# Four networks in a row on 4 x 56 x 56 x 128: spectra with an image in the input's tile, constant products in the later stages, bulk loads behind the first transform

## The chip, the cores and the metric

The kernel runs on one core of a Trainium2 chip, in one launch. A core has five engines that work side by side, each through its own list of instructions in order: TensorE (PE, matrix products; its weight loads are listed as PEld), VectorE (DVE), ScalarE (ACT), GpSimd (POOL) and SyncE (SP, which here only issues transfers). They meet through semaphores. TensorE's accumulators (PSUM) and the working memory (SBUF) hold 128 partitions each. The metric is the device time of an execution in microseconds (us).

## The reference

Four layers are applied to x (4, 56, 56, 128), each as `x = x + layer(groupnorm(x))`. Layer 0 is window attention, attention over all 3,136 tokens of a sample, and an MLP. Layer 1 is a graph layer over all pairs of 56 nodes. Layer 2 takes each of the 56 images of a sample (56 x 128) through a Fourier neural operator; layer 3 is a convolution over rows with sums along both axes. The change lies in layer 2, of which this matters:

```python
xa_n = _inorm(xa, norm_g[0], norm_b[0])                  # each image normalised
k = _fno_layer(xa_n, wK, wKs, bKs, (H // 2, W // 2))     # 32 heads each
q = _fno_layer(xa_n, wQ, wQs, bQs, (H // 2, W // 2))
v = _fno_layer(xa_n, wV, wVs, bVs, (H, W))
...
scores = jnp.einsum('bhtd,bhsd->bhts', qs, ks) / (np.sqrt(ks.shape[-1]).astype(np.float32) * TEMPERATURE)
attn_w = jax.nn.softmax(scores, axis=-1)                 # 56 x 56 per head and sample
out = jnp.einsum('bhts,bhsd->bhtd', attn_w, vs)
...
projd = _fno_layer(out, wP, wPs, bPs, (H, W))
attention = _inorm(projd + xa, norm_g[1], norm_b[1])
an = _inorm(attention, norm_g[2], norm_b[2])
m = _fno_layer(an, wM0, wM0s, bM0s, (H, W), (norm_g[3], norm_b[3]), act=True)
m = _fno_layer(m, wM1, wM1s, bM1s, (H, W), (norm_g[4], norm_b[4]), act=False)
output = _inorm(m, norm_g[5], norm_b[5]) + attention
```

where `_fno_layer` is a two-dimensional Fourier transform, a product with weights on the low frequencies, the transform back, and a skip path.

## The kernel before

**First layers.** Four samples run one after another (`first_layers`): a front (lines named f_, layer 0) and then the edge layer (e_, layer 1, `edge_layer`). The input of a sample lies in the tile xw (128 x 3136 numbers), the edge layer's result in x1. While a sample's front runs, group norm and image norm of the sample before it are done (`normed_images`), and its normalised images are stored to xad and, transposed, to xat in DRAM. For the last sample, number 3, that is left to the next stage, and its images stay in x1.

**Spectra** (`spectra`, L1699). Each sample's images pass a first transform in four quarters (`first_transform`: 28 pairs of thin products, s_pr, L1655; a multiplication by the image's own factor into s_z, L1657, on DVE; a copy on ACT, L1659). `sample_spectra` then makes from s_z the score spectra S and iS (s_ps, L1671, copies on ACT), the skip path's R (s_pr2, L1683) and the value spectra xh (s_px, L1693, copied in turn by ACT and DVE). It is a generator of 13 steps; between its steps the next sample's quarters are put (after steps 2, 5, 7 and 9), and steps of image 3's normalisation (`go_on`). That normalisation has 28 steps of two row statistics each, small products (s_pt, L1572 to L1615), two square roots, and four passes over the tile (`normed`, L1622, through `apply_norm`). The order on TensorE, ACT and DVE here is that of the code. `fill(n)` issues n products of the identity with ones (L1721), whose result nobody reads.

Images 0, 1 and 2 come from xad into tiles s_x2, of which there are two, and each transfer is issued on SP (`images`, L2933). SP takes its transfers in order: images 0 and 1, the store of x1 to x2d, small weights, the score weights (`all_score_weights`) and value weights (`value_weights`), image 2 when a tile is free, then dd, xat, the spectra's reordered copies (apart, q_T, q_Tp) and the first u_d. POOL computes with the weights meanwhile; the products of value weights go out as dd, which `attend` loads again as u_d.

**Score pass** (`attention_weights`, L1811). The samples are paired: bp = 0 is samples 0 and 1, bp = 1 samples 2 and 3. For each pair `seq` has 32 items (16 columns c, n = 0 and 1) and four odd items. `make` prepares an item's tile q_u: on DVE for n = 0 (L1864), on POOL for n = 1 (L1862). `product` (L1877) multiplies it, 16 records on TensorE, into q_acc. `make` runs four items ahead. `collect` adds q_acc to the scores y (L1896). The skip products and the softmax of the first pair are generators in `between`, one step after each item. A softmax step is a reduction, a subtraction, a reduction, a reciprocal and a multiplication on DVE (L1902 to L1911), an exponential on ACT, and transposes on TensorE (q_pt, L1919) that ACT copies to AT.

**Attend** (L1955) multiplies dd into the spectra (u_ud on DVE, L2018; u_up on POOL, L2020) and TensorE sums over AT (u_po, L2023), in 24 turns. Other work is put between, among it the second pair's softmax.

**Outputs** (L2777 on) hold the mixed FNO layers and layer 3. Their instructions are made as operations of a `Plan` and issued in an order written out by hand (OUTPUT_ORDER). The plan only asserts that dependences and the counted buffers are kept; tiles come from `bank()` and `banks()`.

Of the kernel before, what the change touches and what calls it, by code (L numbers as in the profile page):

```python
# [19 lines left out]
P = 128  # L20
# [1531 lines left out]
def normed_images(k, w, st, b, wk, bank, xp, xad, xat):  # L1552
# [48 lines left out]
    nc.vector.tensor_scalar(mean, mean, 0.5, mr[:, 0:1], ALU.mult, ALU.subtract)  # L1601
    nc.vector.tensor_scalar_mul(mean, mean, mr[:, 1:2])
    yield
    nc.vector.tensor_scalar(sq, sq, mr[:, 1:2], mr[:, 1:2], ALU.mult, ALU.mult)
# [37 lines left out]
def first_transform(k, st, b, pools, x, to):  # L1642

    nc = k.nc
    wk, psum = pools

    z = to[b] = wk.tile([P, 33, 2 * HH], F32, name="s_z")
    xf = x.rearrange("p t h -> p (t h)")  # L1650
    for t0 in range(0, HH, 14):
        ps = psum.tile([P, 512], F32, tag="row", name="s_pr")
        for t in range(14):
            for ri in range(2):
                nc.tensor.matmul(ps[64 * ri:64 * ri + 64, t * 33:(t + 1) * 33],  # L1655
                                 xf[:, (t0 + t) * HH:(t0 + t) * HH + 64], k.fw[:, ri, :], start=True, stop=True)
# [41 lines left out]

def spectra(k, w, st, xat, images):  # L1699

# [6 lines left out]
    with ExitStack() as es:  # L1707
# [6 lines left out]
        zs = {}  # L1714
        first = [first_transform(k, st, b, (wk, psum), st.x1 if b == B - 1 else images(b), zs) for b in range(B)]
        idle = tiny.tile([P, 512], F32, name="s_pt")
# [94 lines left out]
def attention_weights(k, I, w, st):  # L1811
# [9 lines left out]
    with ExitStack() as es:  # L1821
# [127 lines left out]
def attend(k, I, w, st, dd, xat, xm, softmax, beside, psum):  # L1949
# [4 lines left out]
    with ExitStack() as es:  # L1954
# [14 lines left out]
        def prepare(turn):  # L1969
# [18 lines left out]
            else:  # L1988
# [15 lines left out]
                 (1, 6): (mixing,), (2, 14): (mixing,), (2, 6): (mixing,), (2, 2): (mixing,), (3, 14): (mixing,)}  # L2004
        late = []
        prepare(0)
        for turn, (g, n, bp) in enumerate(turns):
# [5 lines left out]
            for i in range(2):  # L2013
                for h0, m, e in (shares if turn else first)[left < 16]:
# [6 lines left out]
                    for q in range(m):  # L2021
                        for b2 in range(2):
                            nc.tensor.matmul(po[64 * b2:64 * b2 + 64, :NB],  # L2023
                                             st.AT[:, 8 * i + h0 + q, 2 * bp + b2, :], u[:, b2, q, :],
                                             start=(left == 16), stop=(left == 1))
# [150 lines left out]


class Plan:

# [3 lines left out]
    def __init__(self, **buffers):  # L2183
        self.ops, self.buffers = [], buffers

# [7 lines left out]
    def issue(self, order):  # L2193
# [7 lines left out]
        for n in order:  # L2201
            op = self.ops[n]
            assert all(a.end for a in op.after)
            for b, key in op.takes:
                taken[b].append(key)
                old = len(taken[b]) - 1 - self.buffers[b]
                assert old < 0 or not users[b, taken[b][old]]
            op.run()
            op.end = True
            for g in op.gives:  # L2210
                users[g] -= 1


# [555 lines left out]
def outputs(k, w, st, ys, x2d, xm, out, psum):  # L2769

    tc = k.tc
    with ExitStack() as es:
        pools = Env()
        pools.wk = es.enter_context(tc.tile_pool(name="o_wk", bufs=2))
        opened, taken = [], [0]

        def bank():  # L2777
            return psum.tile([P, 512], F32, tag="b", name="o_b")

        def banks():  # L2780
            taken[0] += 1
            tag, bufs = ("x", 1) if taken[0] % 3 == 0 else ("px", 2)
            return psum.tile([P, 2, 512], F32, tag=tag, name="o_d", bufs=bufs)
        pools.bank, pools.banks = bank, banks
# [19 lines left out]
        for b, op in ((1, wholes[3].spread[0]), (2, wholes[3].factors)):  # L2804
            for p in wholes[b].convolve:
                p.after.append(op)
        plan.issue([int(n) for n in OUTPUT_ORDER.split()])

# [28 lines left out]
def build(k, packs, I, out):  # L2837
# [3 lines left out]
    with ExitStack() as es:  # L2841
# [8 lines left out]
        x1w = x1p.tile([P, HH + 1, HH], F32, name="x1")  # L2850
        x1 = x1w[:, :HH, :]
        dd = dp.tile([3, 4, 2, 16, NB], F32, name="dd")

# [4 lines left out]
        with tc.tile_pool(name="w01", bufs=1) as wp, tc.tile_pool(name="io", bufs=1) as io:  # L2858
            xw = io.tile([P, TOK], F32, name="xw")
            with ExitStack() as pre:  # L2860
# [52 lines left out]
            with small.Else():  # L2913
# [4 lines left out]
                with tc.tile_pool(name="n_x", bufs=2) as xs, tc.tile_pool(name="n_ps", bufs=2, space=PSUM) as psum:  # L2918
                    for b in range(B - 1):
                        xp = xs.tile([P, HH, HH], F32, name="n_x")  # L2920
                        nc.sync.dma_start(xp, x2d[b])
                        for _ in normed_images(k, w2, st, b, io, lambda: psum.tile([P, 512], F32, name="n_ps"), xp,
                                               xad, xat):
                            pass

        x2s = ExitStack()
        x2p = x2s.enter_context(tc.tile_pool(name="x2", bufs=2, side="right"))

        def images(b):
            if b not in loaded:  # L2930
                xp = loaded[b] = x2p.tile([P, HH + 1, HH], F32, name="s_x2")
                for o in (slice(0, 29), slice(29, HH)):
                    nc.sync.dma_start(xp[:, o, :], xad[b, :, o, :])  # L2933
                nc.gpsimd.memset(xp[:, HH, :], 0.0)
            return loaded[b]

        loaded = {}
        for b in range(2):
            images(b)
        nc.sync.dma_start(x2d[B - 1], x1)  # L2940
        l3p = es.enter_context(tc.tile_pool(name="l3", bufs=1))
        load_weights(k, l3p, I, "w3_", w2)
        load_weights(k, l3p, I, "w2_", w2, only=CONV_WEIGHTS)
        st.AbT = l3p.tile([P, 2, HH], F32, name="AbT")
        st.dc = l3p.tile([1, B, HH], F32, name="dc")
        with tc.tile_pool(name="xh", bufs=1) as xp:
            st.xh = xp.tile([112, B, 2, 32, HH], F32, name="xh")
            with tc.tile_pool(name="sp", bufs=1) as sp:
# [4 lines left out]
                with tc.tile_pool(name="g_wk", bufs=1, side="right") as wk:  # L2953
                    all_score_weights(k, I, w2, sp, wk, st)
                    value_weights(k, I, w2, wk, dd)
                    spectra(k, w2, st, xat, images)
                x2s.close()
# [35 lines left out]
```

## Time and profile before

| | us |
|---|---|
| median of 3 runs (least and greatest) | 3463.82 (3462.63 to 3465.51) |
| the profiled execution | 3464.84 |
| its span in the trace | 3463.1 |
| last edge stage ends, images 0 and 1 are issued | 2586.65 |
| first product of the spectra (constant) | 2588.75 |
| first product of the score pass | 2671.28 |
| first product of its second pair | 2733.92 |
| first u_po of attend | 2806.60 |

The span runs from the first instruction to the last; an execution is 1.7 us longer than it. The table's lower rows are starts on TensorE (for the images, on SP's queue), in us from the start of the span. In rows of the profile, `out<-in` are tile names, `x` counts records, and the mean or total follows in us. A product of 32-bit numbers can be more than one record on TensorE: a constant product over 384 columns has two. "Granted clock" (PEclk) is the share of TensorE's full clock that the chip allowed in a stretch, 1.00 being full speed.

### The profile page before, as it was taken

The page shows a single profiled execution, that of the slowest core. Times are in us where ns is not written, and L with a number is a line of the kernel's source. Part 1 is how long each engine was busy: PE and PEld are TensorE (multiplying, and loading weights), DVE is VectorE, ACT ScalarE, POOL GpSimd, SP SyncE. Part 2 cuts the span into 40 slices and gives each one's busy share as a digit, 9 for nine tenths or more (in the row PEclk, how much of TensorE's full clock was granted, in tenths as well). Part 3 has the DMA queues.
Part 4 walks back from the last instruction along what each step waited for, and adds up shares of the span by engine and source line. Part 5 has one row for each costly group of instructions (what it writes and reads, how often), then busy time and mean ns, then how long its engine had stood idle before and what let it go on. Part 6 is the DMA issues. An engine that isn't in the chain of part 4 may idle for free. (4 is left out here: it accounts for less than half of the span.)

```text
span 3463.1 us, 64456 instructions
## 1 busy us (share of the span) xinstructions
PE 3319.0 (96%) x27800; PEld 1425.6 (41%) x27800; DVE 2657.9 (77%) x2555; ACT 2131.1 (62%) x2253; POOL 1285.9 (37%) x796
## 2 busy tenths in 40 slices
PE   7999999999999999999999999999999999999998
PEld 4433333353333435333343443333337433336664
DVE  6588867867888696788859858887794778895776
ACT  4688876668888575788857668887653012215442
POOL 1000007800000491000019400000775778884786
PEclk9999999999999999999999999999999999999999
DMA  2143420024434000444310033442014037743101
GB/s 106 43 94 89 97 54 19 20 53 93 92 91 86 19 1 20 106 103 91 91 42 1 20 81 90 93 97 54 1 40 118 1 87 187 190 115 94 57 20 56
DMA packets 98012, 243.41 MB, mean 70 GB/s; under 512 B 64457, under 2 KB 69833, under 8 KB 92713
## 3 DMA queue, kind: packets, MB, share of 16 engines
q0 software_dynamic: 16128, 102.77, 14.8%
q1 hardware_dynamic: 74872, 123.61, 12.2%
q10 hardware_dynamic: 6720, 12.85, 1.3%
q8 instruction: 220, 3.60, 0.4%
q14 instruction: 72, 0.58, 0.1%
HBM read 79.43 MB, written 31.33 MB: 32 GB/s over the span
## 5 line engine op out<-in xcount | busy, mean ns | idle before, releaser
L830 ACT ACTIVATE f_ring<-f_pm 128x1792 f32<-128x1792 f32 (+1 forms) x764 | 1093.8, 1482 | 226.4 <-PE f_pm L827 179.6
L682 DVE TENSOR_TENSOR f_acc<-f_acc,f_ring 128x1792 f32<-128x1792 f32 x468 | 947.5, 2025 | 190.2 <-ACT f_ring L830 160.0
L827 PE MATMUL f_pm<-f_qT,f_kT 32*128 32x448 f32 x5376 | 722.6, 571 | 9.9 <-ACT f_p L716 4.1
L672 POOL DMA_DIRECT2D f_far<-f_ring x112 | 96.5, 862 | 1328.2 <-ACT f_ring L830 1033.4
L693 PE MATMUL f_pm<-f_ring,f_va 128*32 128x448 f32 (+1 forms) x6304 | 589.4, 490 | 0.0
L1269 POOL TENSOR_TENSOR e_tp<-e_a,e_c 128x1792 f32<-128x1792 f32 (+2 forms) x172 | 480.4, 2831 | 36.7 <-issue 36.7
L1267 DVE TENSOR_TENSOR e_td<-e_a,e_pc 128x1792 f32<-128x1792 f32 (+2 forms) x292 | 478.3, 1703 | 8.8 <-ACT e_c L1255 8.8
L827 PEld LDWEIGHTS f_pm<-f_qT,f_kT 32*128 32x128 f32 x5376 | 260.2, 183 | 411.5 <-ACT f_ring L830 300.3
L693 PEld LDWEIGHTS f_pm<-f_ring,f_va 128*32 128x32 f32 x6304 | 163.8, 109 | 410.1 <-issue 397.8
L1271 ACT ACTIVATE e_tp<-e_tp 128x1792 f32<-128x1792 f32 (+2 forms) x172 | 253.3, 1495 | 98.0 <-POOL e_tp L1269 98.0
L2018 DVE TENSOR_TENSOR u_ud<-u_px,u_d 112x1792 f32<-112x1792 f32 x144 | 263.4, 1863 | 39.7 <-PE u_po L2023 35.1
L2020 POOL TENSOR_TENSOR u_up<-xh,u_d 112x1792 f32<-112x1792 f32 (+1 forms) x72 | 240.9, 3373 | 55.0 <-PE u_po L2023 40.7
L1338 PE MATMUL e_acc<-e_td,t_edge 128*32 128x448 f32 x1952 | 231.6, 542 | 6.6 <-DVE e_td L1267 6.4
L2023 PE MATMUL u_po<-u_ud,AT 112*64 112x448 f32 x1056 | 213.9, 544 | 1.9 <-DVE u_ud L2018 1.9
L1338 PE MATMUL e_acc<-e_tp,t_edge 128*32 128x448 f32 x1184 | 147.9, 543 | 23.7 <-ACT e_tp L1271 23.7
L2023 PEld LDWEIGHTS u_po<-u_ud,AT 112*64 112x64 f32 x1056 | 74.3, 138 | 128.9 <-issue 112.8
L1338 PEld LDWEIGHTS e_acc<-e_td,t_edge 128*32 128x32 f32 x1952 | 61.6, 110 | 142.6 <-issue 93.7
L737 DVE RECIPROCAL f_den<-f_den 128x448 f32<-128x448 f32 x28 | 82.6, 2951 | 44.9 <-ACT f_den L734 44.9
L1862 POOL TENSOR_TENSOR q_u<-iS,q_g 128x1792 f32<-128x1792 f32 x32 | 102.8, 3235 | 22.8 <-PE q_acc L1877 22.8
L813 POOL TENSOR_TENSOR x<-xf,xw 128x343 f32<-128x343 f32 x28 | 25.5, 911 | 224.7 <-DVE xf L802 224.7
L1877 PE MATMUL q_acc<-q_u,S 64*64 64x448 f32 x1024 | 104.4, 552 | 4.4 <-DVE q_u L1864 3.3
L2121 ACT COPY x_ev<-x_po 56x896 f32<-56x896 f32 x32 | 28.8, 900 | 126.9 <-DMA x_xs<-xat 51.1
(525 smaller groups left out, 4579.1 us busy)
## 6 DMA issues: line engine op xcount, KB each, us to landing
f_far<-f_ring POOLq DMA_DIRECT2D x112, 896.0 KB, 6.4
u_d<-dd SPq DMA_DIRECT2D x46, 784.0 KB
f_far<-f_ring SPq DMA_DIRECT2D x28, 896.0 KB
xw<-in_x SPq DMA_DIRECT2D x4, 1568.0 KB
x2d<-x SPq DMA_DIRECT2D x4, 1568.0 KB
xat<-x SPq DMA_DIRECT2D x4, 1568.0 KB
x_xs<-xat ACTq DMA_DIRECT2D x32, 196.0 KB
xm<-x_ev ACTq DMA_DIRECT2D x64, 98.0 KB
```

The costliest lines, as they stand in the source:

```text
L682: nc.vector.tensor_add(e.acc, e.acc, slots(j, c))
L693: nc.tensor.matmul(e.po[heads[h], part], va[o, c, heads[h]], p, start=(c == 0), stop=(c == 23 and part.stop == NB))
L827: nc.tensor.matmul(ss[:, i, :NB], kT[heads[h], c * P:(c + 1) * P], qT[heads[h], blk(j)], start=True, stop=True)
L830: nc.scalar.activation(ring[:, slot:slot + m, :], ss[:, :m, :NB], AF.Exp, scale=scale)
L1267: nc.vector.tensor_tensor(t, am, cm, ALU.max)
L1269: nc.gpsimd.tensor_sub(t, am, cm)
L1271: nc.scalar.activation(tf, tf, AF.Relu)
L1338: nc.tensor.matmul(acc[quarters[r0 + r], :NB], w.S[:, 0, :], t[:, r].rearrange("p l n -> p (l n)"), start=(g == 0), stop=(g == len(turns) ...
L1877: nc.tensor.matmul(acc[bp][i][halves[hb % 2], hb // 2, :NB], x[o], u[o, 8 * hb:8 * hb + 8, :].rearrange("p h t -> p (h t)"), start=first, ...
L2018: nc.vector.tensor_mul(u, bc(px[:, :, :NB], 2, m), dm)
L2020: nc.gpsimd.tensor_mul(u, bc(x, 2, m), dm)
L2023: nc.tensor.matmul(po[64 * b2:64 * b2 + 64, :NB], st.AT[:, 8 * i + h0 + q, 2 * bp + b2, :], u[:, b2, q, :], start=(left == 16), stop=(left ...
```

## The change

1. The tile xw becomes 57 rows high and outlives the first layers. Image 0 is loaded into it from xad when the last sample's front has read it (`first_image`), and image 2 after image 0's first transform. Image 1 has the only s_x2 tile. `first_transform` asks for its tile when it starts.
2. In the spectra, image 0's four quarters stand first, with one fill(4) after the third; the steps of image 3's normalisation are put between the steps of the samples. Its four passes over the tile are done by ACT for sample 3 (`b == B - 1`).
3. `bulk`, called after the first transform, holds the score and value weights, the store x2d and the small weights, in that order on SP; image 2 is ahead of them.
4. The score pass begins with four constant products. In the first pair, POOL's items come one pair later. The first pair's softmax takes its steps at items n with n % 4 == 2 and n > 38 only.
5. Attend begins with four constant products, and has two more in turn 0.
6. In the outputs eleven constant products are issued: with the tile of operation n (FILL_OWN), or with a tile of their own ahead of it (FILL_SPARE).

```diff
     def normed():
         for t in range(0, HH, 14):
-            apply_norm(k, x[:, t:t + 14, :], x[:, t:t + 14, :], mr)
+            if b == B - 1:
+                nc.scalar.activation(x[:, t:t + 14, :], x[:, t:t + 14, :], AF.Identity, bias=t1, scale=mr[:, 1:2])
+            else:
+                apply_norm(k, x[:, t:t + 14, :], x[:, t:t + 14, :], mr)
...
-        fill(3)
-        go_on(28)
-        next(first[0])
-        next(first[0])
-        go_on(1)
-        fill(4)
-        next(first[0])
-        go_on(1)
-        next(first[0])
-        go_on(2)
+        for n in range(4):
+            next(first[0])
+            if n == 2:
+                fill(4)
+        images(2)
+        bulk()
         for b in range(B):
             for n, _ in enumerate(sample_spectra(k, st, b, (wk, psum), zs.pop(b))):
-                go_on(2)
+                go_on(4 if b == 0 and n < 7 else 2 if b and n > 8 else 1)
...
             for c in range(16):
-                seq += [(bp, c, 0, None), (bp, c, 1, None)]
+                seq.append((bp, c, 0, None))
+                if bp or c:
+                    seq.append((bp, c - (not bp), 1, None))
                 if c in (8, 10, 12, 14):
                     seq.insert(len(seq) - 1, (bp, None, c // 2 % 2, c // 12))
+            if not bp:
+                seq.append((bp, c, 1, None))
...
         ahead = 4
+        idle = psum.tile([P, 512], F32, tag="t", name="q_idle", bufs=1)
+        for _ in range(4):
+            nc.tensor.matmul(idle[:, :3 * P], k.ident, bc(k.ones, 1, 3), start=True, stop=True)
...
-            if n >= 3 and between and next(between[0], 0) == 0:
+            if n >= 3 and between and (item[0] == 0 or n % 4 == 2 and n > 38) and next(between[0], 0) == 0:
                 between.pop(0)
...
+        idle = bank()[:, 0, :3 * P]
+        def fill(n):
+            for _ in range(n):
+                nc.tensor.matmul(idle, k.ident, bc(k.ones, 1, 3), start=True, stop=True)
+        fill(4)
         prepare(0)
...
+                    if not turn and left == 15:
+                        fill(2)
...
+FILL_OWN = {42: 1, 82: 1, 330: 1, 743: 2, 748: 2}
+FILL_SPARE = {30: 1, 160: 1, 273: 2}
...
+            if n in FILL_SPARE:
+                self.idle = FILL_SPARE[n]
+                taken["b"].append(("idle", n))
...
+                self.spare()
+            self.idle = FILL_OWN.get(n, 0)
             op.run()
...
+        def filled(t, out):
+            for _ in range(plan.idle):
+                k.nc.tensor.matmul(out, k.ident, bc(k.ones, 1, 3), start=True, stop=True)
+            plan.idle = 0
+            return t
...
         with tc.tile_pool(name="w01", bufs=1) as wp, tc.tile_pool(name="io", bufs=1) as io:
-            xw = io.tile([P, TOK], F32, name="xw")
...
+            def first_image():
+                nc.sync.dma_start(xi[:, :HH, :], xad[0])
+                nc.gpsimd.memset(xi[:, HH, :], 0.0)
...
                 front(k, w0, xw, xf, x1, st)
+                if to is None:
+                    first_image()
                 edge_layer(k, w1, x1, st)
...
-        x2p = x2s.enter_context(tc.tile_pool(name="x2", bufs=2, side="right"))
+        x2p = x2s.enter_context(tc.tile_pool(name="x2", bufs=1, side="right"))
...
-                xp = loaded[b] = x2p.tile([P, HH + 1, HH], F32, name="s_x2")
+                xp = loaded[b] = xi if b == 2 else x2p.tile([P, HH + 1, HH], F32, name="s_x2")
...
-        loaded = {}
-        for b in range(2):
-            images(b)
-        nc.sync.dma_start(x2d[B - 1], x1)
+        loaded = {0: xi}
+        images(1)
         l3p = es.enter_context(tc.tile_pool(name="l3", bufs=1))
-        load_weights(k, l3p, I, "w3_", w2)
-        load_weights(k, l3p, I, "w2_", w2, only=CONV_WEIGHTS)
...
+                    def bulk():
+                        all_score_weights(k, I, w2, sp, wk, st)
+                        value_weights(k, I, w2, wk, dd)
+                        nc.sync.dma_start(x2d[B - 1], x1)
+                        load_weights(k, l3p, I, "w3_", w2)
+                        load_weights(k, l3p, I, "w2_", w2, only=CONV_WEIGHTS)
```

More of the change, by code (lines that the diff above doesn't have):

```diff
@@ L1602, in normed_images @@
     nc.vector.tensor_scalar_mul(mean, mean, mr[:, 1:2])
+    if b == B - 1:
+        nc.vector.scalar_tensor_tensor(t1, mr[:, 0:1], -1.0, mr[:, 1:2], ALU.mult, ALU.mult)
     yield
@@ L1621, in normed @@
         for t in range(0, HH, 14):
-            apply_norm(k, x[:, t:t + 14, :], x[:, t:t + 14, :], mr)
+            if b == B - 1:
+                nc.scalar.activation(x[:, t:t + 14, :], x[:, t:t + 14, :], AF.Identity, bias=t1, scale=mr[:, 1:2])
+            else:
+                apply_norm(k, x[:, t:t + 14, :], x[:, t:t + 14, :], mr)
             if t < 42:
@@ L1649, in first_transform @@
     z = to[b] = wk.tile([P, 33, 2 * HH], F32, name="s_z")
-    xf = x.rearrange("p t h -> p (t h)")
+    xf = x().rearrange("p t h -> p (t h)")
     for t0 in range(0, HH, 14):
@@ L1696, in sample_spectra, with spectra @@
         yield
-def spectra(k, w, st, xat, images):
+def spectra(k, w, st, xat, images, bulk):
     nc, tc = k.nc, k.tc
@@ L1714, in spectra @@
         zs = {}
-        first = [first_transform(k, st, b, (wk, psum), st.x1 if b == B - 1 else images(b), zs) for b in range(B)]
+        first = [first_transform(k, st, b, (wk, psum), lambda b=b: st.x1 if b == B - 1 else images(b), zs)
+                 for b in range(B)]
         idle = tiny.tile([P, 512], F32, name="s_pt")
@@ L2175, in conv_weights @@
     yield
+FILL_OWN = {42: 1, 82: 1, 330: 1, 743: 2, 748: 2}
+FILL_SPARE = {30: 1, 160: 1, 273: 2}
 class Plan:
     def __init__(self, **buffers):
-        self.ops, self.buffers = [], buffers
+        self.ops, self.buffers, self.idle, self.spare = [], buffers, 0, None
     def add(self, engine, cost, run, after=(), takes=(), gives=(), lag=0.0, table=None):
@@ L2207, in issue @@
                 assert old < 0 or not users[b, taken[b][old]]
+            if n in FILL_SPARE:
+                self.idle = FILL_SPARE[n]
+                taken["b"].append(("idle", n))
+                users["b", ("idle", n)] = 0
+                old = len(taken["b"]) - 1 - self.buffers["b"]
+                assert not users["b", taken["b"][old]]
+                self.spare()
+            self.idle = FILL_OWN.get(n, 0)
             op.run()
@@ L2211, in issue @@
                 users[g] -= 1
+            assert not self.idle
 def half_sample(k, w, st, plan, b, half, whole, pools, rows, x2d, xm):
@@ L2775, in outputs @@
         opened, taken = [], [0]
+        def filled(t, out):
[3 more added lines that the diff above has]
+            return t
         def bank():
-            return psum.tile([P, 512], F32, tag="b", name="o_b")
+            t = psum.tile([P, 512], F32, tag="b", name="o_b")
+            return filled(t, t[:, :3 * P])
         def banks():
@@ L2782, in banks @@
             tag, bufs = ("x", 1) if taken[0] % 3 == 0 else ("px", 2)
-            return psum.tile([P, 2, 512], F32, tag=tag, name="o_d", bufs=bufs)
+            t = psum.tile([P, 2, 512], F32, tag=tag, name="o_d", bufs=bufs)
+            return filled(t, t[:, 0, :3 * P])
         pools.bank, pools.banks = bank, banks
@@ L2806, in outputs @@
                 p.after.append(op)
+        plan.spare = bank
         plan.issue([int(n) for n in OUTPUT_ORDER.split()])
@@ L2851, in build @@
         x1 = x1w[:, :HH, :]
+        xwp = x1s.enter_context(tc.tile_pool(name="xw", bufs=1, side="right"))
+        xi = xwp.tile([P, HH + 1, HH], F32, name="xw")
+        xw = xi[:, :HH, :].rearrange("p t h -> p (t h)")
         dd = dp.tile([3, 4, 2, 16, NB], F32, name="dd")
@@ L2924, in build @@
                             pass
+                first_image()
         x2s = ExitStack()
[L2927 removed]
+        x2p = x2s.enter_context(tc.tile_pool(name="x2", bufs=1, side="right"))
         def images(b):
             if b not in loaded:
[L2931 removed]
+                xp = loaded[b] = xi if b == 2 else x2p.tile([P, HH + 1, HH], F32, name="s_x2")
                 for o in (slice(0, 29), slice(29, HH)):
                     nc.sync.dma_start(xp[:, o, :], xad[b, :, o, :])
[L2934 removed]
+                if b < 2:
+                    nc.gpsimd.memset(xp[:, HH, :], 0.0)
             return loaded[b]
[L2937 to L2940 removed]
+        loaded = {0: xi}
+        images(1)
         l3p = es.enter_context(tc.tile_pool(name="l3", bufs=1))
[L2942 to L2943 removed]
         st.AbT = l3p.tile([P, 2, HH], F32, name="AbT")
@@ L2953, in build @@
                 with tc.tile_pool(name="g_wk", bufs=1, side="right") as wk:
-                    all_score_weights(k, I, w2, sp, wk, st)
-                    value_weights(k, I, w2, wk, dd)
-                    spectra(k, w2, st, xat, images)
+                    def bulk():
[4 more added lines that the diff above has]
+                        load_weights(k, l3p, I, "w2_", w2, only=CONV_WEIGHTS)
+                    spectra(k, w2, st, xat, images, bulk)
                 x2s.close()
```

## The prediction

> **What bounds the kernel now.** I read the page's busy shares first, then the chain, then a table of the stretches that the change touches, then TensorE's waits there, and the granted clock last.
>
> ```profile
> span 3463.1 us, 64456 instructions
> PE 3319.0 (96%) x27800; PEld 1425.6 (41%) x27800; DVE 2657.9 (77%) x2555; ACT 2131.1 (62%) x2253; POOL 1285.9 (37%) x796
> ```
>
> TensorE is busy 96% of the span, so a gain must come from work taken off it, from its few idle stretches, or from its clock. Windows over the five stretches that the diff touches (start:end and length in us; busy time of PE, PEld, DVE, ACT, POOL; granted clock; DMA share; GB/s): spectra, first half of the score pass, second half, attend, outputs.
>
> ```profile
> 2588.00:2668.00 80.00, 75.89 (x1222) 65.25 (x1222) 37.20 (x113) 31.19 (x69) 35.27 (x53) 0.96 0.47 143
> 2668.00:2733.00 65.00, 61.51 (x816) 29.59 (x816) 46.16 (x26) 2.60 (x5) 57.04 (x19) 0.97 0.14 33
> 2733.00:2801.50 68.50, 61.58 (x560) 27.60 (x560) 50.17 (x32) 5.96 (x8) 45.90 (x15) 0.95 0.00 1
> 2801.50:3122.50 321.00, 316.19 (x1768) 117.84 (x1768) 277.94 (x172) 68.49 (x103) 267.01 (x91) 0.99 0.64 156
> 3122.50:3463.00 340.50, 314.71 (x2234) 205.02 (x2232) 226.41 (x398) 144.36 (x207) 222.59 (x136) 0.98 0.20 58
> ```
>
> The reader is to see a busy TensorE at a clock below 1.00: part of that busy time is slow time. What it waits for, by total, times and longest:
>
> ```profile
> PE q_pt L1919 <- DVE y L1911: 5.9, 1, 5.9
> PE q_acc L1877 <- DVE q_u L1864: 3.3, 1, 3.3
> PE u_po L2023 <- POOL u_up L2020: 2.4, 1, 2.4
> PE u_po L2023 <- DVE u_ud L2018: 1.9, 1, 1.9
> ```
>
> And the clock in short windows, same columns:
>
> ```profile
> 2608.00:2612.00 4.00, 2.91 (x50) 2.67 (x50) 1.37 (x5) 0.82 (x3) 2.99 (x8) 0.83 1.02 411
> 2612.00:2616.00 4.00, 4.00 (x38) 3.94 (x35) 1.36 (x3) 1.11 (x2) 3.80 (x6) 0.50 0.66 257
> 2672.00:2676.00 4.00, 4.00 (x28) 1.61 (x22) 4.00 (x3) 0.00 (x0) 4.00 (x2) 0.57 0.77 171
> 2744.00:2748.00 4.00, 0.98 (x4) 0.69 (x4) 3.97 (x3) 0.00 (x0) 2.02 (x1) 0.50 0.00 0
> 3400.00:3402.00 2.00, 2.00 (x16) 0.76 (x12) 0.26 (x2) 0.30 (x1) 2.00 (x2) 0.50 0.00 0
> 3416.00:3418.00 2.00, 2.00 (x4) 0.96 (x3) 1.41 (x4) 0.00 (x0) 2.00 (x2) 0.54 0.00 0
> ```
>
> Narrowing such windows, every change of clock lies a whole number of 3.413 us from every other. Half speed holds in 2610.67–2617.4, 2672.09–2675.5, 2743.75–2750.55, 2805.2–2812.0, 3399.1–3402.5 and 3416.2–3419.6. A half-speed window in which TensorE is the bound costs 1.7 us, half of 3.41.
>
> **Rule against row.** The Trainium skill, "TensorE: Matmul & The Clock Gate", section "Why this matters for your kernels", says that one idle window throttles the clock and warns of idle gaps above some 3 us. By it only the gap before 2747 would go cold, and constant products in short gaps would be useless work. The trace differs: in the windows ahead of the drops TensorE was busy 2.08 (2607.26), 0.83 (2668.69), 0.78 (2740.37), 0.97 (2801.81), 2.33 (3395.71) and 2.15 us (3412.78); others with 1.71 to 2.47 stayed fast. I take the row: a window about half filled is at risk. By the rule, the clock terms below (3.4 + 1.2 + 1.7 = 6.3) drop out, and the sum is −14.2 instead of −20.5.
>
> **1. Spectra, −8.** These lines (start, length, engine, line, operation) are the beginning now:
>
> ```profile
> 2588.75 2.17 PE L1721 MATMUL s_pt<-c_ones,t_shared 128*128 128x384 f32 x6 [0.94 <-PE e_idle L1298]
> 2591.72 3.46 PE L1655 MATMUL s_pr<-t_images,s_x 128*64 128x33 f32 x112 [0.80 <-DMA s_x<-xad]
> ```
>
> Six constant records wait out image 0's transfer, issued at 2586.65 when the edge stage ends. The change sends images 0 and 1 (1,568 KB each) under the last edge stage. Earlier batches load as much there, so I cost that at 0; uncovered it is some 5 us (2586.65 to 2591.72).
>
> Removed: fill(3), 2.17, the 0.80 wait, and the normalisation of image 3 ahead of the second quarter. New work of TensorE from 2588.7: 16 quarters at 1.755 (28.1), one fill(4) at 2.8, 256 columns' s_px at 0.103 (26.3), s_ps 4 x 1.75 (7.0), s_pr2 4 x 1.0 (4.0), norm products 1.0: 69.2. The hand-over from the last s_z to s_ps was 0.73 and stays; about 1 us of small waits I keep. It ends at 2659.6, against 2667.97: −8.3. I take −8, since four normalisations move to ACT (its 128x896 copy took 0.95, 128x448 0.53, so some 0.83 each) among the xh copies that TensorE waits for. In the list 3.4 comes from the two slow windows and 1.1 from `s_pt L1615 <- DVE s_sq`.
>
> What moves: image 2 now waits for the third and fourth quarter (about 2596.5, 2598.5), and is needed around 2617; it took about 5 us when issued alone, so it is hidden. SP's bulk loads stand behind it. POOL's weight work (2605.6 to 2642.9) must be complete for the score pass and dd before u_d's loads (2672): at a start of 2600 to 2606 there are 20 us to spare. The store xat waits for ACT (about 2635); behind it on SP stand apart, q_Tp and later u_d, the first needed 25 us later. The new normalisation spreads POOL- and DVE-side waits over samples 0 and 1. Bounds: −4 (image 2 or ACT late) to −10 (all small waits gone).
>
> **2. Beginning of the score pass, −1.2.** Four q_idle products fill the 3.3 us in which q_u is made: 2.8 us, ending about 0.1 after q_u is ready. The slow window (2672.09, 1.7) goes; TensorE then catches up with DVE's second product (0.4 lost). Bounds −1.7 to +1.
>
> **3. Second half, −9.3.** DVE's softmax for the first half of the heads is issued at every item in a row, so the transposes (q_pt) wait 5.9 at 2741 to 2747 and the next 3.4 run slow. The change gives it eight turns, at items 42 to 70, and no POOL-side product is delayed by them. Work for TensorE: 512 product records at 0.094 (48.1), odd items 4 x 1.66 (6.6), transposes 2.3, small waits 1: 58.2 against the 67.45 from 2733.9 to 2801.35. DVE does 30 us of products in this time (15 of 2.02) plus the softmax, about 4.6 per pair of b2 (reduce 1.08, subtract 1.09, reduce 1.08, reciprocal 0.25, multiply 1.09): stepped by hand, it stays 1.8 us ahead. The one multiply beside POOL took 2.68 instead of 1.09; two such use that lead up. Bounds −4.5 to −10.
>
> **4. Attend, 0.** fill(4) waits for the second collect (DVE, 2803.43) and would end at 2806.3, where u_po starts now (2806.60); fill(2) ends at 2808.1. DVE gives the next u_ud then, and at 2814.7 TensorE waits for DVE in both orders, so a faster clock is not kept. Bounds −0.5 to +1.
>
> **5. Outputs, −2.** The eleven extra products go into gaps of 0.66 to 1.34 us, each 0.70, two pairs slightly over (0.3). 3416's slow window goes (1.7), and I count half of 3399's at 0.6. Bounds −3 to +3.
>
> The third item of the score pass's order (POOL's second product one pair later) changes who waits by less than 0.3; its cover is `ahead = 4`.
>
> **Sum**: −8 −1.2 −9.3 +0 −2 = −20.5 on the profiled execution, 3464.84 (span 3463.1 and 1.7 around it): 3444.3. The median of the runs shown is 1.0 lower: 3443.3, put at **3443.5**.
>
> **Rivals.** (B) DVE becomes the bound in the second half: its share there is 50.17 of 68.50, and in 58 us it would be 86%. For it: 2.68 where 1.09 was enough. Against it: the 1.8 us lead. Gain 4.5 instead of 9.3: 3448.5. (C) The spectra gain half, because image 2, ACT's copies or the first load (DMA share 1.02 at 2608) are late: 3447.5. (D) The output products push the chain: each on the path costs 0.7, and the phase of the 3.413 us grid shifts by the gains upstream, so other gaps may fall into one window. Outputs +3 instead of −2: 3448.5. (E) The slower end: the spectra run at half speed throughout, because thin products (33 and 112 columns) count too little. Place: 2588 to 2660, 21 windows at 1.7. It decides from 12 windows (20.5 / 1.7); 16 make it slower by 0.2%, 21 give 3443.5 + 36 = 3479. For it: the window with 2.08 busy at 2607 fell, and fill(3) is gone ahead of the transforms. Against it: 2617 to 2668, the same mix, 15 windows at full clock. That images still arrive late, so that the first part does not do what it says, would cost 5 and is within (C).
>
> **Numbers.** Forecast 0.62, B 0.13, C 0.12, D 0.06, E 0.03, smaller unnamed losses that leave less than 0.2% 0.04. About 6.9 us (0.2%) is what a measurement can tell from no change. B, C and D alone stay faster; two together leave 10 to 12 of gain. So faster 0.93, same 0.04, slower 0.03. The forecast's bounds (spectra −10, outputs −3, second half −10) reach 3438; B to D end at 3448.5, and half of another miss at 3452: range 3438 to 3452.
>
> **What would show it.** Right: s_pr first at 2588.7 with no constant product ahead, first s_ps near 2599; clock 1.00 in 2588–2660 and at the score pass's beginning; no q_pt wait above 1 us; second half about 58; the stage's end near 2783; outputs about 338. Wrong: a wait of s_pr for image 2, of s_ps for ACT's normalisation, of q_acc for q_u at items 42 to 70, or a half-speed window behind a gap in the outputs that was fast before.

## The result and the profile after

| | before | changed |
|---|---|---|
| median of 14 runs (least and greatest), us | 3464.64 (3461.41 to 3465.73) | 3456.99 (3451.65 to 3464.92) |
| span of the profiled execution, us | 3463.1 | 3453.9 |
| mean granted clock there | 0.993 | 0.996 |

The ratio of the runs is 0.9981, with a 95% interval of 0.9973 to 0.9988. The change gains 7.7 us where 20.5 were forecast. The first lines of the page of the changed kernel:

```profile
span 3453.9 us, 64526 instructions
PE 3325.2 (96%) x27836; PEld 1429.8 (41%) x27836; DVE 2659.6 (77%) x2552; ACT 2134.5 (62%) x2257; POOL 1285.0 (37%) x795
```

The same five stretches as a table of windows of the changed kernel, with the columns of the table before:

```profile
2588.00:2665.00 77.00, 71.68 (x1220) 61.62 (x1218) 36.85 (x111) 34.98 (x74) 34.78 (x57) 1.00 0.50 129
2665.00:2729.50 64.50, 62.85 (x826) 30.30 (x826) 46.82 (x27) 2.38 (x5) 56.28 (x19) 1.00 0.03 8
2729.50:2790.00 60.50, 59.54 (x560) 27.26 (x560) 49.17 (x31) 5.96 (x8) 48.15 (x15) 1.00 0.00 1
2790.00:3112.50 322.50, 319.67 (x1780) 119.99 (x1780) 278.10 (x172) 68.58 (x103) 267.22 (x91) 0.99 0.64 155
3112.50:3453.90 341.40, 323.43 (x2256) 209.59 (x2254) 226.59 (x398) 144.16 (x207) 222.55 (x136) 0.98 0.20 57
```

In this trace the clock is 1.00 in the first three stretches, as hoped, and the second half of the score pass has lost its 8 us of waiting and slow time. Attend and the outputs are no shorter. TensorE's waits of the changed kernel from the spectra to attend:

```profile
PE s_pr L1660 <- issue: 3.4, 3, 1.5
PE x_po L2020 <- DVE y L1902: 2.2, 1, 2.2
PE q_acc L1883 <- DVE y L1902: 1.1, 1, 1.1
PE q_acc L1883 <- DVE q_u L1870: 0.9, 1, 0.9
```

The wait of q_pt is gone. New at the top is a wait of s_pr for "issue", that is, for nothing that the profile shows. By stage, from start to start of TensorE's products:

| stage | forecast | before | changed | difference |
|---|---|---|---|---|
| start to the last edge product | 0 | 2583.7 | 2585.1 | +1.4 |
| to the first product of the scores | -8 | 87.5 | 83.1 | -4.4 |
| first pair | -1.2 | 62.6 | 61.3 | -1.3 |
| second pair, to its last product | -9.3 | 66.9 | 59.9 | -7.0 |
| to the last product of attend | 0 | 321.4 | 322.7 | +1.3 |
| to the end | -2 | 340.8 | 341.9 | +1.1 |

(The first row's times are positions in the span. The rows are rounded and add up to -8.9; unrounded, they and the spans differ by 9.1.)

### The profile page after: what moved, and what is told of

Same layout as the page of the kernel before. It is cut to its first block, busy times and chain, and to the rows that moved or that the text cites. A ratio compares the mean times of both kernels' runs of the same rounds, so it can differ in the third digit from the quotient of the medians.

```text
span 3453.9 us, 64526 instructions
## 1 busy us (share of the span) xinstructions
PE 3325.2 (96%) x27836; PEld 1429.8 (41%) x27836; DVE 2659.6 (77%) x2552; ACT 2134.5 (62%) x2257; POOL 1285.0 (37%) x795
## 5 line engine op out<-in xcount | busy, mean ns | idle before, releaser
L802 DVE SCALAR_TENSOR_TENSOR xf<-f_pm,t_first,xf 128x392 f32<-128x392 f32 x28 | 17.5, 626 | 113.3 <-PE f_pm L800 113.3
```

## The experiments

Times are medians, with the number of runs, and the ratio to runs of the kernel before on the same chip.

| kernel | us (runs) | ratio and 95% interval |
|---|---|---|
| xw_right_only | 3480.43 (5) | 1.0053 (1.0039 to 1.0066) |
| norm_on_act | 3452.13 (6) | 0.9964 (0.9952 to 0.9976) |
| before_norm_act | 3460.66 (21) | 0.9990 (0.9983 to 0.9996) |
| fill_spread | 3457.38 (13) | 0.9988 (0.9976 to 0.9999) |
| softmax_every | 3462.67 (13) | 0.9999 (0.9991 to 1.0007) |
| softmax_only | 3459.40 (22) | 0.9994 (0.9984 to 1.0005) |
| changed kernel again | 3457.71 (14) | 0.9989 (0.9978 to 1.0000) |
| no_output_fill | 3461.46 (21) | 0.9993 (0.9984 to 1.0002) |
| no_begin_fill | 3457.11 (14) | 0.9981 (0.9973 to 0.9989) |
| both_mended | 3449.90 (6) | 0.9958 (0.9946 to 0.9970) |
| softmax_and_norm | 3455.66 (12) | 0.9973 (0.9964 to 0.9982) |
| mended_no_begin | 3450.69 (5) | 0.9961 (0.9947 to 0.9975) |

### The first layers, which the sum did not hold

Laid beside each other, the two traces show that the changed kernel begins 1.4 us ahead (one half-speed window fewer near the start) and loses 0.7 at the beginning of each of samples 1, 2 and 3, and 0.7 more in a half-speed window at 1321.6. The timeline of the kernel before at sample 1 (start, length, engine, line, operation, tiles, idle before it):

```profile
679.67 1.41 POOL L340 MEMSET w_qd<- 128x1568 f32 x1
680.15 1.14 DVE L193 TENSOR_SCALAR w_xg<-xw,mr 128x392 f32<-128x392 f32 x1
...
681.91 0.62 DVE L225 TENSOR_SCALAR w_qd<-w_mm,t_first 32x392 f32<-32x392 f32 x1 [0.62 <-PE w_mm L375]
```

And of the changed kernel:

```profile
678.19 1.41 POOL L340 MEMSET w_qd<- 128x1568 f32 x1
678.68 3.61 DVE L193 TENSOR_SCALAR w_xg<-xw,mr 128x392 f32<-128x392 f32 x1
...
680.60 1.41 POOL L340 MEMSET w_qd<- 128x1568 f32 x1
682.21 0.60 DVE L225 TENSOR_SCALAR w_qd<-w_mm,t_first 32x392 f32<-32x392 f32 x1
```

DVE's normalisation of the third group reads xw. In both it starts half a microsecond behind POOL's first long memset, with more memsets right behind that one. Before, it is through 0.2 us after the first; now it lasts past the next long one too (680.60 + 1.41 = 682.01), with 0.3 us to spare. The Trainium skill, "SBUF — State Buffer", section "SBUF: two separate sides", says that GpSimd and certain instructions of DVE share a pair of ports as an exclusive lock, and that the one that starts second is fully blocked. The 3.61 us, against 0.48 for the same instruction elsewhere in this trace, agree in kind: DVE comes second and is held up. That it ends 0.3 us behind a memset, less than its own 0.48, leaves open how fully it was blocked, the more so as POOL's times are rough. Why DVE gets in after one memset with the tile in its old place, and only after the whole row of them in the new one, the page does not say and the runs do not show. The first experiment moved the tile alone.

```diff
+        xws = ExitStack()
+        xwp = xws.enter_context(tc.tile_pool(name="xw", bufs=1, side="right"))
+        xi = xwp.tile([P, HH + 1, HH], F32, name="xw")
+        xw = xi[:, :HH, :].rearrange("p t h -> p (t h)")
...
-            xw = io.tile([P, TOK], F32, name="xw")
...
+        xws.close()
         x2s = ExitStack()
```

> The kernel before with one edit: the tile xw lies where the change puts it (57 rows, beside x1), and is given up after the first layers; images, orders and constant products are as before. Theory of the tile's place: at the beginning of samples 1, 2 and 3 the first DVE normalisation beside POOL's memsets takes 3.6 us instead of 1.14, as in the changed kernel's trace, each costs TensorE 0.7 net, and the time is 2 us above the kernel before (ratio 1.0006). Rival, that this was chance of the one profile: 1.14 stays and the time is within 1 us of before.

The 3.61 came at all three samples, and in every further trace with the tile in its new place in which DVE does this normalisation; the last edge product stood at 2586.5, 2.7 later than before. So the place (or that of the tiles that shifted with it) is the cause. But the time rose by 16 us, not 2: from the first s_ps to the scores it took 80.2 us instead of 69.2, with 20.5 us at half speed instead of 6.8. If TensorE was the bound there, the extra 13.7 us at half speed cost 6.8 of these 11 us; most of the rest is in two waits (3.5 us instead of 1.1 for DVE's s_sq, 2.1 instead of 0.5 for ACT's xh). In its trace DVE's small operations run beside POOL's weight work there, and the first of its four passes over image 3 took this long, where the kernel before has 0.68 to 2.11 for each of the four:

```profile
2620.98 8.96 DVE L193 TENSOR_SCALAR x<-x,s_mr 128x784 f32<-128x784 f32 x1
```

The changed kernel has these passes on ACT and is spared that. Why this version's POOL and DVE meet so badly was not tried further. The mend gives the normalisation to ACT, which stood idle 1.7 to 3.5 us there:

```diff
-            if g < 2:
+            if g < 3:
                 nc.scalar.activation(out, x, AF.Identity, bias=shift, scale=mr[:, 1:2])
```

> The changed kernel with the third group's normalisation at the beginning of each front on ACT instead of DVE. Theory that DVE's 3.6 us there (it cannot start while POOL's memsets follow one another) is the price of the tile's new place: the first w_qd comes 1.5 us earlier, each of samples 1 to 3 begins about 0.7 us sooner on TensorE and no longer draws a half-speed window; last edge product 2 to 3 us earlier than in the changed kernel, time 2 to 4 us below it at equal phase. Rival, that ACT or the next stage waits as long: last edge product within 0.5 us.

The last edge product came at 2581.6 instead of 2585.1, 3.5 earlier, and the median at 3452.13, 5 below the changed kernel, somewhat more than expected. At sample 1 DVE's first w_qd starts 2.4 us after ACT's first w_xg, where the changed kernel has 4.1. No half-speed window falls at the beginnings of samples 1 to 3.

The same edit in the kernel before:

> The kernel before with the third group's normalisation on ACT. Theory that DVE's 3.6 us is the price of the new place: here that instruction takes 1.14 and the next 2.08, so ACT wins less than in the changed kernel: last edge product at most 1.5 us earlier than before's 2583.7 at equal phase, time 0 to 2 us lower. Rival, that the old place pays as much through its second instruction (2.08): 3 us earlier, as in the changed kernel.

Here the last edge product moved from 2583.7 to 2582.5, while the median fell by 3.5, more than the expectation's 2. The old place paid as well, through the 1.14 and a second one of 2.08. Neither sentence of the expectation holds whole, and the medians (3.5 us here, 5 there) are too close to say by how much the places differ. The traces of all versions together say it better. The last edge product stands at 2586.2 on the mean of the nine with DVE and the new place (2585.1 to 2586.9), and at 2583.7 and 2585.7 in the two with DVE and the old one; with ACT it is 2582.0 on the mean in both places (three traces and two). So the move costs about 1.5 us, and giving the work to ACT takes away that and 2.7 us that the old place cost already.

### The first transform

The changed kernel's first transform on TensorE:

```profile
2590.35 3.48 PE L1660 MATMUL s_pr<-t_images,xw 128*64 128x33 f32 x113 [1.18 <-issue]
2595.33 1.82 PE L1660 MATMUL s_pr<-t_images,xw 128*64 128x33 f32 x55 [1.51 <-issue]
2597.09 2.85 PE L1727 MATMUL s_pt<-c_ones,t_shared 128*128 128x384 f32 x8
2599.86 1.83 PE L1660 MATMUL s_pr<-t_images,xw 128*64 128x33 f32 x56
```

It stops for 1.5 us behind 113 products, that is 226 instructions with their weight loads, gone through in 3.5 us. The Trainium skill, "Runtime: NRT & Kernel Launch", section "Instruction fetch mechanics", has an engine's program refilled in blocks of 256 instructions, a taken branch breaking the prefetch, and the crossing of a block mostly hidden. This place follows the end of the kernel's one If, and at 31 ns per product the crossing is not hidden. The trace's transfers bear that out. A queue of kind "instruction" (q8) brings 220 packets of 16,384 bytes each; at that page's 256 instructions a block they are, by estimate, 56,320 instructions, about TensorE's 55,672 products and weight loads and far more than any other engine has. One of them lands at 2593.96, and the product after the stop begins 1.4 us later. All eight traces with this order stop behind product 113. The stop lasts 1.5 to 2.2 us, but in all eight its end lies 1.2 to 1.5 us behind the landing of such a packet. Six of the eight also have one or two half-speed windows in the transform. The experiment keeps the four constant products and spreads them:

```diff
-            if n == 2:
-                fill(4)
+            if n < 2:
+                fill(2)
```

> The changed kernel with its four constant products of the first transform placed two after the first quarter and two after the second, instead of four after the third. Theory that TensorE runs out of instructions, since thin products go through at 31 ns each: the idle 1.5 us between the second and third quarter goes, from the first s_pr to the first s_ps 10.6 us instead of 12.1, the time 1.5 to 2 us below the changed kernel at equal clock. Rival, that transfers or the s_z product hold the third quarter: the gap stays at 1.5 us or moves to a named wait, and the time stays.

In its trace:

```profile
2591.16 1.83 PE L1660 MATMUL s_pr<-t_images,xw 128*64 128x33 f32 x56 [1.21 <-issue]
2592.92 1.56 PE L1727 MATMUL s_pt<-c_ones,t_shared 128*128 128x384 f32 x4
2594.40 2.18 PE L1660 MATMUL s_pr<-t_images,xw 128*64 128x33 f32 x56
2596.52 1.56 PE L1727 MATMUL s_pt<-c_ones,t_shared 128*128 128x384 f32 x4
2598.00 3.46 PE L1660 MATMUL s_pr<-t_images,xw 128*64 128x33 f32 x112
```

Nothing idles between the quarters; inside the second, 0.3 us are left of the stop, again ending 1.2 us behind the landing of a packet. The transform takes 11.0 us to s_ps instead of 12.1, where 10.6 was expected, and the stretch from the edge stage to the scores 81.1 instead of 83.1. The three traces with this edit have no half-speed window in the transform and 10.8 to 11.0 us to s_ps; the eight of the changed kernel and its versions without the edit have 12.1 to 16.0. So the supply of instructions is what held TensorE here. The median, though, did not fall (3457.38 against 3456.99): three of the 13 runs lay at 3469 to 3472, with a mean clock of 0.990 or 0.991. At equal mean clock, by the slope given below, the runs lie only 0.5 us lower, no more than their scatter; where the time is given back stays open.

### The softmax

```diff
-            if n >= 3 and between and (item[0] == 0 or n % 4 == 2 and n > 38) and next(between[0], 0) == 0:
+            if n >= 3 and between and next(between[0], 0) == 0:
```

> The changed kernel with the first pair's softmax taking a step at every item again. Theory that the spread softmax is what shortens the second pair: the wait of q_pt for DVE (5 to 6 us) returns, and from the second pair's first product to the last collect it takes 66 to 67 us instead of about 59; time 7 to 9 us above the changed kernel at equal clock. Rival, that the clock or POOL's order made the gain: at most 3 us above.

The wait returned, as long as before, in TensorE's list of waits:

```profile
PE q_pt L1925 <- DVE y L1917: 5.9, 1, 5.9
```

The second pair took 66.9 us instead of 59.9; the median rose by 5.7 over the changed kernel's (5.3 over fill_spread's on the same chip), somewhat less than expected. The condition alone, put into the kernel before:

> The kernel before with one part of the change: the first pair's softmax takes its steps at items 42 to 70 only. Theory: the second pair takes about 60 us instead of 66.9, the half-speed windows at 2744 are gone, the rest is as before; time 7 us below the kernel before (ratio 0.998), which is the whole gain of the change. Rival, that the other parts bring as much as this one: 3 us or less below.

Its second pair took 59.9, by this window from the second pair's first to its last product and a little beyond:

```profile
2736.00:2799.00 63.00, 59.58 (x562) 27.29 (x562) 51.32 (x33) 6.23 (x9) 48.83 (x16) 1.00 0.02 7
```

So the 7 us of this stage are its own. The median fell by 4.8, and five of its 22 runs lay at 3469 to 3480: between the expectation's two cases, and the interval reaches 1.

### Where the clock's windows fall

> The changed kernel itself once more. Theory of the clock's phase: of its half-speed windows only those at the start, at the end and perhaps at the first normalisations of samples 1 to 3 recur; the 10.2 us at 3284 and the 3.4 at 2793 of its first profile lie elsewhere or are missing, with the same instructions in the same order; single runs lie 10 us or more apart and follow the mean clock at 2.4 to 3.4 us per 0.001. Rival, that each window belongs to a place in the program: the same list within 1 us.

The second trace had the windows at 1322.0, 2793.1 and 3284.6, each within 0.5 us of the first, as the rival said. But its grid also lay within 0.4 us of the first's (the windows start at 1.01 instead of 0.65, modulo 3.413), so this did not decide. Two more traces of the same program:

> The changed kernel a third time, for one more trace. Its two traces so far have the clock's grid at 0.65 and 1.01 us (start of the half-speed windows, modulo 3.413) and the same windows. Theory that place and phase decide together: if the grid lies more than 1 us from these, the list differs: the 10.2 us at 3284 and the 3.4 at 2793 are shorter or gone, others may be there. Rival, place alone: the same list whatever the phase.

> The changed kernel a fourth time, for the same question as the third: at a phase away from 0.65 to 1.01 the list of half-speed windows differs (place and phase decide), or it is the same (place alone). In both cases the span is that of the others plus or minus half of the difference in half-speed time.

They came at phases 0.20 and 1.21 (one run each, 3458.59 and 3455.23 us). Windows of the first trace, at four places:

```profile
2596.00:2600.00 4.00, 4.00 (x51) 2.62 (x49) 0.64 (x1) 0.58 (x1) 3.90 (x8) 1.00 0.88 255
3284.50:3288.00 3.50, 3.50 (x13) 2.26 (x14) 3.50 (x4) 1.23 (x3) 3.50 (x2) 0.50 1.13 226
3288.00:3292.00 4.00, 4.00 (x16) 2.47 (x14) 2.81 (x4) 0.00 (x0) 3.92 (x4) 0.50 0.00 0
3391.00:3394.00 3.00, 3.00 (x34) 1.78 (x33) 1.44 (x6) 0.30 (x1) 2.30 (x2) 1.00 0.02 5
```

And of the fourth, which runs some 1.6 us later through the program:

```profile
2596.00:2600.00 4.00, 2.69 (x56) 2.41 (x57) 0.89 (x2) 0.58 (x1) 3.96 (x8) 0.84 0.40 105
3284.50:3288.00 3.50, 3.50 (x29) 2.79 (x28) 2.97 (x5) 2.84 (x5) 3.50 (x2) 1.00 0.59 129
3288.00:3292.00 4.00, 4.00 (x28) 2.50 (x25) 4.00 (x5) 0.00 (x0) 3.92 (x4) 1.00 0.53 92
3391.00:3394.00 3.00, 3.00 (x18) 1.33 (x14) 0.76 (x3) 0.30 (x1) 3.00 (x3) 0.50 0.03 5
```

The clock column (the third from the end) is the point: the 10.2 us at half speed at 3284 are missing, and others stand at 2598.8 and 3390.6 in their stead. The third trace has 6.8 us at 2597.7 and 10.2 at 3287.2. Place and phase decide together: certain places are at risk, and an execution's phase picks among them. The phase that counts is the one against the program, not against the start of the span. From the last product of attend to the next boundary of the grid it is 1.56 to 1.70 us in the first three traces of the changed kernel and in that of fill_spread. These four have the 10.2 us at half speed, 172.2 to 172.4 us behind that product, and no other trace has them. In eleven further traces the boundary comes after 0.10 to 0.69 or after 3.16 us, and in all of them 3.4 us at half speed stand 276.2 to 277.2 us behind it, with the constant products of the outputs or without. The sixteenth trace comes last here, with 0.92 us. So here the phase settles which of the two places drops.

Over the 14 first runs the time fell by 2.4 us for each 0.001 of mean clock (correlation -0.94, worked out from the list of runs); over 294 runs of the thirteen kernels, each taken from its own kernel's mean, by 2.7 (-0.94).

How long a spell can last is seen in a trace with a mean clock of 0.991, of softmax_and_norm (below), in its outputs:

```profile
3287.50:3292.00 4.50, 4.50 (x19) 3.00 (x18) 4.50 (x5) 1.67 (x5) 4.50 (x3) 0.50 0.91 178
3292.00:3296.00 4.00, 4.00 (x16) 2.54 (x14) 2.55 (x4) 0.00 (x0) 3.81 (x3) 0.50 0.01 4
3296.00:3300.00 4.00, 4.00 (x16) 2.43 (x13) 2.13 (x5) 0.00 (x0) 4.00 (x3) 0.50 0.00 0
```

TensorE is busy throughout and at half speed, for 17.1 us in all; its outputs took 349.7 us where others have 339.6 to 342.0.

### The constant products

Without those of the outputs:

```diff
-FILL_OWN = {42: 1, 82: 1, 330: 1, 743: 2, 748: 2}
-FILL_SPARE = {30: 1, 160: 1, 273: 2}
+FILL_OWN = {}
+FILL_SPARE = {}
```

> The changed kernel without the eleven constant products of the outputs. The prediction's step (they keep a window fast): outputs 2 us longer, time 2 us above the changed kernel. Rival, that half-speed windows fall by the phase of the clock's grid wherever the products are thin: the time is within 1.5 us of the changed kernel's median, its runs spread as widely (some 10 us), and in each run the time follows the mean clock at about 2.4 us per 0.001.

The trace's outputs took 340.1 us; with the products, the changed kernel's four traces have 339.8 to 342.0. At like phases, with the grid's next boundary 0.36 to 0.69 us behind attend, four traces with the products have 339.6 to 339.9 and four without have 339.6 to 340.8, so there they are worth about a microsecond at most. The median, though, was 4 us higher, and the runs lay between 3453 and 3471, along the mean clock: 8 of the 21 took over 3465 us, where the changed kernel has 2 of 28. That the products save time in other phases is possible; no trace shows where, and it stays open.

Without those at the two beginnings:

```diff
-        for _ in range(4):
-            nc.tensor.matmul(idle[:, :3 * P], k.ident, bc(k.ones, 1, 3), start=True, stop=True)
...
-        fill(4)
         prepare(0)
...
-                    if not turn and left == 15:
-                        fill(2)
```

> The changed kernel without the four constant products at the score pass's beginning and the six in attend. The prediction's steps: the score pass's first pair 1.2 to 1.3 us longer (62.6 instead of 61.3) with a half-speed window behind the wait for q_u, attend as long as before; time 1 to 2 us above the changed kernel at equal phase. Rival, that they only add work: time at or below the changed kernel, 61.3 stays.

By chance its grid lay at 0.15, beside the third trace's 0.20. Up to the second pair the two differ as forecast: the first pair took 62.6 us against 61.3. From there attend took 321.6 in both. But the version without the products ended at 3456.7 and the other at 3456.8, because the 1.8 us that the products had won by the end of attend were lost again in the outputs (341.8 with them against 339.9, with 10.2 us of half speed at 3287 against 3.4 at 3393 for the version without). The medians do not differ.

### The mends together

> The changed kernel with the constant products spread over the first transform and the third group's normalisation on ACT. If both causes are right and add: edge stage's end 2 to 3 us and the first s_ps a further 1.5 us earlier than in the changed kernel; time 4 to 5 us below it, near 3452. Rival, that a gain upstream is given back by other half-speed windows: median within 2 us of the changed kernel.

The median is 3449.90, 7 below the changed kernel and 14 below the kernel before, more than the 4 to 5 expected; in its trace the last edge product stands at 2582.9 and the first s_ps 10.8 us behind the first s_pr. It has the lowest median of all versions, on six runs.

> The kernel before with the spread softmax and the third group's normalisation on ACT, without the change's other parts. If the image part, the order of the spectra and the constant products bring something of their own once the front's price is taken away on both sides, this lies 3 to 6 us above the changed kernel with both mends (3449.9), at 3453 to 3456: spectra 86 to 87 us from the last edge product to the score pass instead of 83. Rival, that they bring nothing: 3450 to 3451.

3455.66: the softmax and the front's mend alone bring some 8 us, so the images, the spectra's order and the constant products bring about 6 more; how these three share it was not tried. From the edge stage to the scores it took 86.6, as expected, against 82.8.

> The changed kernel with both mends and without the constant products at the beginnings of the score pass and of attend. If these products bring the 1.3 us that the first pair shows: 1 to 2 us above the version with both mends, near 3451.5. Rival, that they give back what they gain (the score pass's first product waits for them): equal or lower, 3448 to 3450, with a narrower spread.

3450.69 against 3449.90: five and six runs cannot tell them apart. Its greatest was 3451.13, the other's 3454.71.

## Why the prediction was wrong

The direction was right and the time outside the range: 3456.99 (0.19% faster), where 3443.5 and at most 3452 had been said. Of the 11.4 us between the sum (-20.5) and the trace (-9.1), the spectra hold 3.6, the outputs 3.1, the second pair 2.3, the first layers 1.4 and attend 1.3. Point by point:

1. **"The change sends images 0 and 1 under the last edge stage ... so I cost that at 0."** The images were hidden, and s_pr waited for no transfer. What failed is that the step's price was looked for in transfers only. The tile for it had to move, and the move cost 0.7 us at each of three samples, and more where it drew a half-speed window. Term: 0, measured +1.4 net of 1.4 won by phase at the start. Moving a tile was not among the edits that I priced.
2. **Spectra, -8: no term for TensorE standing still without a wait.** The work was priced nearly right: 70.5 us were measured for 69.2, the 16 quarters 28.2 for 28.1. Only s_px was too cheap, 27.4 for 26.3, since 0.103 is its rate in an unbroken row of 64. What the sum put at nothing are the two stops of 1.5 and 0.7 us for "issue" between the thin products (the third of the list's three, 1.2 us, stood as 0.9 in front of the old fill). 2.2 of stops, 1.1 of s_px and half a microsecond of smaller things make up what is missing. The small waits came to the 1.0 that was kept for them. Image 2 and the bulk loads came in time, and no stall of q_u, dd or u_d came from the moved loads; ACT's four passes took 1.0 us each for 0.83, with a wait of 0.6 for iS behind them. That the clock held 1.00 here was in part luck of the phase: the third and fourth traces have 6.8 and 3.4 us at half speed.
3. **First pair, -1.2**: right (-1.3), and shown by removing the products.
4. **Second pair, -9.3**: the mechanism was right, the size too large. The mis-sized term is "512 product records at 0.094 (48.1)": they took 50.0 us, 0.098 each, at full clock (the sum's parts, moreover, add up to 58.0 and not to 58.2). The small waits were 0.9 (one q_u) for 1, so DVE's lead of 1.8 us did run out once; the wait of 1.1 for the collect stands ahead of the pair:

```profile
2729.48 26.81 PE L1883 MATMUL q_acc<-q_u,S 64*64 64x448 f32 x272 [1.13 <-DVE y L1902]
```

5. **Attend, 0**: +1.3 in the first two traces and 0 to 0.5 at other phases (321.4 to 321.9 in the further traces with these products). The 1.3 comes from a half-speed window on the four constant products themselves, here in the first trace and in the third:

```profile
2792.14 4.51 PE L2020 MATMUL x_po<-c_ones,t_shared 128*128 128x384 f32 x8 [2.22 <-DVE y L1902]
2796.09 2.82 PE L2020 MATMUL x_po<-c_ones,t_shared 128*128 128x384 f32 x8 [2.21 <-DVE y L1902]
```

   The first u_po of the kernel before stands at 2803.77; 2806.60 is its first from DVE. So there was less room for these products than the sum took.
6. **Outputs, -2**: +1.1 in the first trace and -1.0 in the fourth. This is the step that failed in kind. The sum took the half-speed windows of one trace as fixed to their gaps, removed those whose gap was filled, and put none elsewhere. Rival D had the right mechanism (the phase of the grid shifts), with a price of 5 us at the gaps with products; the 5.1 us (half of 10.2) came at 3284, where nothing had been changed. Nor need the products be what removed 3416's window: softmax_only, without them and at nearly the phase of the kernel before, has none there either.

The rule of the Trainium skill ("TensorE: Matmul & The Clock Gate", "Why this matters for your kernels") that I weighed against the rows, by which an idle window throttles the clock, does not cover these traces either: in the window ahead of 2792.8 TensorE was busy 1.19 us. But my own reading, that a half filled window is at risk, was too narrow as well (last section).

Rival B did not happen: DVE did not become the bound. C happened, through another mechanism than the three it named. E, half speed through the whole spectra, happened in none of the changed kernel's four traces; its first transform does draw one or two such windows in two of them.

## What to carry to other kernels

One trace tells where the clock can drop, not where it will. The grid's phase differs from execution to execution, so cost half-speed windows as an average over phases, and compare versions by stages at full clock and by many runs. When a tile moves, look at every instruction that reads it beside GpSimd, however far from the edit. Before packing thin products behind a branch, count instructions per microsecond, not only columns, and look at the trace's instruction packets.

## What was not expected of the hardware

- A full window can be followed by a slow one. In the changed kernel TensorE was busy all of this window (33 records, weight loads 3.37 us), and the next three were at half speed:

```profile
3280.87:3284.28 3.41, 3.41 (x33) 3.37 (x30) 2.67 (x6) 3.38 (x5) 3.41 (x3) 1.00 0.02 5
3284.28:3287.70 3.42, 3.42 (x14) 2.44 (x15) 3.42 (x5) 1.45 (x4) 3.42 (x2) 0.50 1.14 229
```

  Most of its products are thin, 7 or 64 columns:

```profile
3280.82 1.06 PE L2397 MATMUL o_b<-o_r,slot 128*128 128x7 f32 x8
3281.73 4.14 PE L2317 MATMUL o_d<-t_images,o_t 128*128 128x64 f32 x28
```

  So what the clock's control counts is not the profile's busy time; what it counts, no run here shows. Constant products put into gaps cannot cure a place that has no gap.
- The same DVE instruction took 0.48, 1.14, 2.08, 3.61 us (and a larger one 0.68 or 8.96), with POOL at work beside it.
- TensorE stopped for 1.5 us after 226 thin instructions in 3.5 us, with no semaphore and no transfer of data to wait for; it went on 1.4 us after a packet of instructions had landed.
